# A last group's attention with its own buffers, and contexts dealt out over four steps instead of three

## The chip, the cores and the metric

The kernel runs on one core of a Trainium2 chip. The metric is the device time of one execution in microseconds (us). Times in the profile count from the first instruction of the profiled execution. Engines are called PE (TensorE), PEld (its weight loads), DVE (VectorE), ACT (ScalarE), POOL (GpSimd) and SP (the queue that issues all transfers here).

## The reference

Two layers follow each other on x of 16 batches x 128 tokens x 512 channels; a second input, the context, has the same shape. The first layer is an RWKV block: layer norm, token shift with five learned mixes, projections r, k, v, w, g, a decaying state recurrence per head, group norm, gate, output projection Wo, and a feed-forward part with Wfk, Wfr, Wfv. The second layer is cross attention of each batch with its context:

```python
Mn = conv1x1(Wn, bn, inorm(x_c))
Mm = conv1x1(Wm, bm, inorm(x_s))
A = softmax(einsum('bct,bcs->bts', Mn, Mm), axis=-1)
Ml = conv1x1(Wl, bl, x_s)
Mo = einsum('bcs,bts->bct', Ml, A)
return conv1x1(Wo, bo, Mo) + x_c
```

Here the token index is the channel of the convolution (128) and the 512 channels are positions, so that the scores of one batch are 512 x 512. All arithmetic is in 32-bit floats.

## The kernel before, in words

The 16 batches form 8 groups of two (g = 0 to 7, `n` = 2). The work on a group is cut into stages, each a Python generator that traces a piece and yields: B (line 227: first norm and mixes), B2 (line 268: projections), R (line 358: the recurrence), C (line 568: output projection, second norm, feed-forward: the "output block"), X (line 759: load of the prepared context) and L (line 810: cross attention, two `stageLb` at line 772, one for each batch). The projected context of each batch, Mm and the values side by side, does not depend on the first layer. `context` (line 732) computes it early, and stores it in DRAM (`mvD`); X loads it later.

Steps set the order (line 845 on). In step s, group g is in the stage whose offset in `OFF` (line 27) is s - g: B, B2, R, C, then L and X. So group 0's output block is traced in step 3, group 1's in step 4. `interleave` (line 823) merges the streams of a step by a key, start delay (`DLY`, line 29) plus progress. The contexts of the groups that `EARLY` (line 30) lists for a step are a stream with delay 1 (line 857): they come after most of that step's other work. The last group (g = 7) has streams of its own in step 10: `stageCb` and `stageLb` for each batch (lines 847 to 850).

What is traced is then scheduled by the framework: a planner walks through its own estimate of time and gives each engine a fixed queue, taking what is ready, first the work that was traced first. A tile gets a buffer of its tag when one is free; an instruction that writes it waits until the previous owner's readers are done. So the tags tie stages together:

- In `stageLb` (line 772) for each of four blocks of 128 score rows (`tt`): scores `pS` (line 785), their negated maximum (787), exp into `e` (789), reciprocal (790), scaling (791), four transposes into `pA` (794), and the copy into `AT` (797), which holds two blocks. After every second block `pO` (803) multiplies AT with the values, and line 805 adds the result to x; line 807 stores the batch. `e` has two buffers, `AT` one, the normalized input `l1n` one (line 727), for both batches and all groups. PSUM banks are given by `T` (line 47): tags bx, c and lv have two banks, ls and la one. In the last group batch 0 takes c for pS, ls for pA and lv for pn and pO; batch 1 takes lv, la and bx.
- `context` (line 732) takes xs in yT or xk2 (by batch), its result MVe in xcT or sx2, the normalized copy in `e`, and the banks ls and la. `stageC` uses yT, xk2, xcT and sx2 too (lines 574 to 587), each with one buffer, and kk in yT (line 615).

Of the kernel before, what the change touches and what calls it, by code (L numbers as in the profile page):

```python
# [7 lines left out]
FP = mybir.dt.float32  # L8
# [11 lines left out]
G = B // n  # L20
# [6 lines left out]
OFF = [0, 1, 2, 3, 4, 4]  # L27
ORDER = [3, 4, 2, 1, 0, 5]
DLY = [-0.2, 0.2, 0.0, 0.4, 0.8, 0.4]
EARLY = {0: [0, 1], 1: [2, 3], 2: [4, 5, 6, 7]}  # L30
LASTX = 2


# [1 line left out]
def rwkv_xattn_kernel(ctx: ExitStack, tc: tile.TileContext, a: dict, out: bass.AP):  # L35
# [5 lines left out]
    sb = ctx.enter_context(tc.tile_pool(name="sb", bufs=2))  # L41
    sb1 = ctx.enter_context(tc.tile_pool(name="sb1", bufs=1))
# [4 lines left out]
    def T(tag, g=None, last=None):  # L47

        if g == G - 1 and last:
            tag = last  # L50
        return dict(tag=tag, bufs=PSB[tag])
# [72 lines left out]
    def rownorm(dst, xap, tag, how, ssum=None):  # L124

        sm = lambda nm, w=1: small.tile([128, w], FP, name=nm, tag=tag + nm)
        rs, nb = sm("rs"), sm("nb")
        lin = lambda o, i, scale, bias: nc.vector.tensor_scalar(o, i, scale, bias, ALU.mult, ALU.add)  # L128
        if how == "dve":
            st6, mv = sm("st6", 6), sm("mv", 2)  # L130
            nc.vector.bn_stats(st6, xap)
            nc.vector.bn_aggr(mv, st6)
            lin(nb, mv[:, 0:1], -1.0, 0.0)
            lin(rs, mv[:, 1:2], 1.0, EPS)
        else:
            if ssum is None:
                ssum = sm("su")
                nc.scalar.activation(dst, xap, AF.Identity, accum_out=ssum)
            lin(nb, ssum, -1.0 / E, 0.0)
            sq = sm("sq")  # L140
            nc.scalar.activation(dst, xap, AF.Square, bias=nb, accum_out=sq)
            lin(rs, sq, 1.0 / E, EPS)
        D["pow"] = nc.gpsimd.tensor_tensor(rs, rs, mhalf[:, 0:1], ALU.pow).ins  # L143
        nc.vector.tensor_tensor(nb, nb, rs, ALU.mult)
        nc.scalar.activation(dst, xap, AF.Identity, bias=nb, scale=rs)
# [33 lines left out]
    def center_wv():  # L179
        for m2 in range(2):  # L180
            wvs = sb.tile([128, 2, 512], FP, name="wvs", tag="wb")
            nc.sync.dma_start(out=wvs, in_=a["Wv"][m2])
            wv = wvs.rearrange("p m (h j) -> p (m h) j", j=16)
            mj = sb1.tile([128, 64], FP, name="mj", tag="AT")
            nc.vector.tensor_reduce(mj, wv, AX.X, ALU.add)
# [541 lines left out]
    def inorm(xap, tag, how, ssum=None, tile_=dict(tag="l1n", bufs=1)):  # L727
        xn = sb.tile([128, 512], FP, name="l1n", **tile_)
        rownorm(xn, xap, tag, how, ssum)
        return xn  # L730
# [21 lines left out]
    def stageE(gs):  # L752

        for g in gs:
            for b in range(n):
                context(g, b)
                yield
# [14 lines left out]
    def stageLb(g, b):  # L772
        d = D[g]
        xb = d["x"][b]
        mv = d["MV"][b]
        Mm, Vc = mv[:, 0:512], mv[:, 512:1024].rearrange("p (c t) -> p c t", c=4)
        xh = inorm(xb, "xh", "act", d["ssum"][b])
        pn = ps.tile([128, 512], FP, name="pn", **T("ls", g, ("lv", "bx")[b]))
        nc.tensor.matmul(pn, lhsT=WnT, rhs=xh, start=True, stop=True)
        Mn = sb.tile([128, 512], FP, name="Mn")  # L780
        nc.scalar.activation(Mn, pn, AF.Identity, bias=l1b[:, 0:1])
        for tt in range(4):
            tsl = slice(128 * tt, 128 * tt + 128)
            pS = ps.tile([128, 512], FP, name="pS", **T("ls", g, ("c", "lv")[b]))
            nc.tensor.matmul(pS, lhsT=Mn[:, tsl], rhs=Mm, start=True, stop=True)  # L785
            nm = small.tile([128, 3], FP, name="nm")
            nc.vector.tensor_reduce(nm[:, 0:1], pS, AX.X, ALU.max, negate=True)  # L787
            e = sb.tile([128, 512], FP, name="e")
            nc.scalar.activation(e, pS, AF.Exp, bias=nm[:, 0:1], accum_out=nm[:, 1:2])  # L789
            nc.vector.reciprocal(nm[:, 2:3], nm[:, 1:2])  # L790
            nc.scalar.activation(e, e, AF.Identity, scale=nm[:, 2:3])  # L791
            pA = ps.tile([128, 4, 128], FP, name="pA", **T("la", g, ("ls", "la")[b]))
            for sc in range(4):
                nc.tensor.transpose(pA[:, sc], e[:, 128 * sc : 128 * sc + 128], ident)  # L794
            if tt % 2 == 0:
                AT = sb1.tile([128, 4, 256], FP, name="AT")
            nc.scalar.copy(AT[:, :, 128 * (tt % 2) : 128 * (tt % 2) + 128], pA)  # L797
            if tt % 2 == 0:
                yield
                continue  # L800
            pO = ps.tile([128, 256], FP, name="pO", **T("la", g, ("lv", "bx")[b]))
            for sc in range(4):
                nc.tensor.matmul(pO, lhsT=Vc[:, sc], rhs=AT[:, sc], start=sc == 0, stop=sc == 3)  # L803
            sl = slice(128 * tt - 128, 128 * tt + 128)
            nc.vector.scalar_tensor_tensor(xb[:, sl], pO, cb, xb[:, sl], ALU.add, ALU.add)  # L805
            yield
        nc.sync.dma_start(out=out[n * g + b], in_=xb)
        yield

    def stageL(g):  # L810
        gens = [stageLb(g, b) for b in range(n)]
        while gens:
            for q in list(gens):
                for _ in range(2):
                    try:
                        next(q)
                    except StopIteration:
                        gens.remove(q)
                        break
                yield  # L820
# [24 lines left out]
    for step in range(G + max(OFF)):  # L845
        streams = []
        if step == G + 2:
            for b in range(n):
                streams.append((stageCb(G - 1, b), 6, 0.4 + 0.1 * b, (7 + b, G - 1)))
                streams.append((stageLb(G - 1, b), 3, 1.4 + 0.1 * b, (9 + b, G - 1)))  # L850
        for k in ORDER:
            for g in range(G):
                if step_of(k, g) == step and not (g == G - 1 and k in (3, 4)):
                    streams.append((ST[k][0](g), ST[k][1], DLY[k], (k, g)))
        if step in EARLY:
            gs = EARLY[step]
            streams.append((stageE(gs), 2 * len(gs), 1, (6, step)))
        interleave(streams)
# [71 lines left out]
```

## Time and profile before

| what | value |
|---|---|
| median of 3 runs (lowest, highest) | 971.24 us (967.41, 981.34) |
| profiled execution: its own time, its span | 969.33 us, 967.5 us |
| mean granted TensorE clock | 0.981 |
| busy: PE, DVE, ACT, POOL | 93%, 67%, 52%, 6% of the span |
| DMA | 134.04 MB, mean 139 GB/s |
| context loads (line 737) | 16, issued from 13.5 to 128.8 us |
| context stores (line 749) | 16, issued from 23.8 to 157.6 us |
| last group's attention, first norm to last add | 922.9 to 964.5 us |

The span is from the first to the last instruction; the execution's own time has some start and end around it. A group of the profile gives the number of instructions, their mean duration and what ended the idle time of their engine. "Busy tenths" are 40 equal slices of the span. The chain that ended last goes back from the last instruction, each time to what released it. A matmul of 32-bit floats can have two records, so that one score product shows as x2.

### The profile page before, as it was taken

The numbers are of one execution on the slowest core, as the hardware profiler recorded it, in microseconds if no ns is written. First come the engines' busy times: TensorE is split into PE (matmuls) and PEld (weight loads), VectorE is DVE, ScalarE is ACT, GpSimd is POOL, SyncE is SP. The second block draws the span as 40 slices with busy tenths as digits, with TensorE's granted clock in tenths as the row PEclk, the third lists the DMA queues.
The fourth block names the chain that finished last, engine by engine and source line by source line (L and its number), as shares of the span: only waits on it lengthen the run. The fifth ranks groups of instructions, "written<-read, shape, count | busy, mean of one in ns | idle before, by whom it ended". The sixth has DMA issues, their size and how long they took to land.

```text
span 967.5 us, 19263 instructions
## 1 busy us (share of the span) xinstructions
PE 898.5 (93%) x7556; PEld 613.0 (63%) x7556; DVE 644.3 (67%) x1599; ACT 500.4 (52%) x1057; POOL 59.2 (6%) x95
## 2 busy tenths in 40 slices
PE   4889999998989999999999999999989998997985
PEld 3666767667554867576756677585846565754643
DVE  5787677946586668875787578755784595942322
ACT  4675273443366445564565445734564265654544
POOL 5111010000000000010000000000000000000000
PEclk9999999999999999999999999999999999998998
DMA  6566647355413635253444524553445323344410
GB/s 200 182 239 215 200 154 247 96 158 190 142 55 72 206 123 179 60 173 110 140 115 132 190 86 131 147 182 102 131 112 145 139 66 113 96 155 142 152 44 23
DMA packets 77612, 134.04 MB, mean 139 GB/s; under 512 B 33825, under 2 KB 43681, under 8 KB 77520
## 3 DMA queue, kind: packets, MB, share of 16 engines
q1 hardware_dynamic: 77522, 132.81, 44.5%
q8 instruction: 60, 0.98, 0.4%
q14 instruction: 30, 0.25, 0.1%
HBM read 104.45 MB, written 22.04 MB: 131 GB/s over the span
## 4 chain that ended last, share of the span: by engine, by line
PE 64%; DVE 18%; ACT 7%; DMA 6%; SPq 3%; issue 2%; POOL 0%; DVEq 0%; ACTq 0%; POOLq 0%
PE ptk L594 14%; PE pj L224 11%; PE pv L331 5%; PE pj L621 5%; PE pO L803 4%; PE pl L456 4%; PE pS L785 4%; DVE PP L394 3%; PE pA L794 2%; PE ptl L674 2%; SPq L425 2%; DVE xm L289 2%; PE pu L505 1%; DVE xm L290 1%; PE po L533 1%
## 5 line engine op out<-in xcount | busy, mean ns | idle before, releaser
L224 PE MATMUL pj<-xm,wb 128*128 128x256 f32 x768 | 179.4, 386 | 2.9 <-DVE xm L289 2.8
L224 PEld LDWEIGHTS pj<-xm,wb 128*128 128x128 f32 x768 | 145.3, 193 | 28.3 <-issue 5.7
L143 POOL TENSOR_TENSOR rs<-rs,mhalf 128x1 f32<-128x1 f32 x64 | 40.8, 644 | 619.2 <-DVE rs L128 605.0
L785 PE MATMUL pS<-MV,Mn 128*128 128x512 f32 x112 | 62.9, 644 | 9.1 <-ACT e L789 5.2
L789 ACT ACTIVATE e<-pS,nm 128x512 f32<-128x512 f32 x64 | 44.3, 693 | 50.1 <-DVE nm L787 49.8
L787 DVE TENSOR_REDUCE nm<-pS 128x1 f32<-128x512 f32 x64 | 43.5, 685 | 40.1 <-PE pS L785 39.9
L803 PE MATMUL pO<-AT,MV 128*128 128x256 f32 x224 | 58.4, 399 | 1.9 <-ACT AT L797 1.9
L289 DVE TENSOR_TENSOR xm<-px,sx 128x512 f32<-128x512 f32 x80 | 53.6, 681 | 7.6 <-PE px L286 7.5
L331 PE MATMUL pv<-wb,xm 128*128 128x512 f32 x128 | 57.5, 597 | 0.2 <-DMA wb<-wvc 0.2
L797 ACT COPY AT<-pA 128x512 f32<-128x512 f32 x64 | 37.4, 585 | 39.1 <-PE pA L794 34.7
L791 ACT ACTIVATE e<-e,nm 128x512 f32<-128x512 f32 x64 | 46.4, 730 | 18.7 <-DVE nm L790 18.7
L290 DVE TENSOR_TENSOR xm<-xm,xaT 128x512 f32<-128x512 f32 x80 | 54.4, 684 | 0.5
L803 PEld LDWEIGHTS pO<-AT,MV 128*128 128x128 f32 x224 | 43.1, 198 | 17.8 <-issue 7.1
L621 PE MATMUL pj<-xk,wb 128*128 128x256 f32 x224 | 52.4, 383 | 0.0
L594 PE MATMUL ptk<-wb,kk 128*128 128x512 f32 x112 | 51.4, 596 | 0.9 <-DMA wb<-in_Wfv_dram 0.9
L456 PE MATMUL pl<-KX,r 128*32 128x128 f32 x1536 | 48.6, 274 | 3.3 <-DMA KX<-ks 3.0
L594 PE MATMUL ptk<-wb,sx 128*128 128x512 f32 x112 | 50.8, 598 | 0.0
L594 PE MATMUL ptk<-wb,yT 128*128 128x512 f32 x112 | 49.8, 596 | 0.8 <-DVE nm L790 0.8
L456 PEld LDWEIGHTS pl<-KX,r 128*32 128x32 f32 x1536 | 40.8, 110 | 14.1 <-issue 8.8
L794 PEld LDWEIGHTS pA<-ident,e 128*128 128x128 f32 x256 | 30.0, 141 | 30.6 <-issue 14.0
L805 DVE SCALAR_TENSOR_TENSOR x<-pO,cb,x 128x256 f32<-128x256 f32 x32 | 15.4, 480 | 49.5 <-PE pO L803 49.3
L286 PE MATMUL px<-sk,w2s 98*128 98x256 f32 x160 | 41.7, 356 | 5.4 <-ACT sk L264 2.0
(201 smaller groups left out, 1709.9 us busy)
## 6 DMA issues: line engine op xcount, KB each, us to landing
wb<-in_Wk_dram SPq DMA_DIRECT2D x16, 512.0 KB, 4.6
mvD<-MVe SPq DMA_DIRECT2D x16, 512.0 KB, 4.1
wb<-in_Wr_dram SPq DMA_DIRECT2D x16, 512.0 KB, 3.4
wb<-wvc SPq DMA_DIRECT2D x16, 512.0 KB, 3.6
wb<-in_Wg_dram SPq DMA_DIRECT2D x16, 512.0 KB, 4.2
wb<-in_Wo_dram SPq DMA_DIRECT2D x14, 512.0 KB, 3.4
wb<-in_Wfk_dram SPq DMA_DIRECT2D x14, 512.0 KB, 3.5
MV<-mvD SPq DMA_DIRECT2D x14, 512.0 KB, 3.8
```

Of the source, the lines that this page charges most:

```text
L224: nc.tensor.matmul(pj[:, m], lhsT=wb[:, m, cc, :], rhs=xm[:, cc], start=cc == 0, stop=cc == 3)
L289: nc.vector.tensor_tensor(xm[:, sl], px.rearrange("p c (b t) -> p c b t", b=n), sx[:, sl], ALU.mult)
L290: nc.vector.tensor_tensor(xm[:, sl], xm[:, sl], xaT[:, sl, :, 1:129], ALU.add)
L331: nc.tensor.matmul(pv, lhsT=xm[:, m, b], rhs=wbs[m // 2][:, m % 2], start=m == 0, stop=m == 3)
L456: nc.tensor.matmul(t[cs, 128 * cc : 128 * cc + 128], lhsT=r[:, cc, b, cs], rhs=KX[:, n * cc + b, :, 16 * c : 16 * c + 16], start=True, sto ...
L594: nc.tensor.matmul(pt, lhsT=act[:, m, b], rhs=wbs[m // 2][:, m % 2], start=m == 0, stop=m == 3)
L621: nc.tensor.matmul(pj[:, m], lhsT=wb[:, m, cc, :], rhs=xk2[:, cc], start=cc == 0, stop=cc == 3)
L785: nc.tensor.matmul(pS, lhsT=Mn[:, tsl], rhs=Mm, start=True, stop=True)
L789: nc.scalar.activation(e, pS, AF.Exp, bias=nm[:, 0:1], accum_out=nm[:, 1:2])
L791: nc.scalar.activation(e, e, AF.Identity, scale=nm[:, 2:3])
L794: nc.tensor.transpose(pA[:, sc], e[:, 128 * sc : 128 * sc + 128], ident)
L803: nc.tensor.matmul(pO, lhsT=Vc[:, sc], rhs=AT[:, sc], start=sc == 0, stop=sc == 3)
```

## The change

Two edits are made together. In the last group each batch's `stageLb` takes other buffers: the normalized input goes to tag vt (two buffers), `e` to xm for batch 0 and k for batch 1 (two buffers each), `AT` to at for batch 0 and w for batch 1 (one each). These tags belong to stages that the last group has left by then. All other groups keep e, AT and l1n. And the contexts, which were computed in steps 0 to 2 for 2, 2 and 4 groups, are computed in steps 0 to 3 for 1, 2, 3 and 2 groups. What is computed stays the same, and no instruction is added or taken away.

```diff
-EARLY = {0: [0, 1], 1: [2, 3], 2: [4, 5, 6, 7]}
+EARLY = {0: [0], 1: [1, 2], 2: [3, 4, 5], 3: [6, 7]}
...
-        xh = inorm(xb, "xh", "act", d["ssum"][b])
+        own = lambda tag, *rest: dict(tag=rest[b]) if g == G - 1 else dict(tag=tag)
+        xh = inorm(xb, "xh", "act", d["ssum"][b], *([dict(tag="vt")] if g == G - 1 else []))
...
-            e = sb.tile([128, 512], FP, name="e")
+            e = sb.tile([128, 512], FP, name="e", **own("e", "xm", "k"))
...
-                AT = sb1.tile([128, 4, 256], FP, name="AT")
+                AT = sb1.tile([128, 4, 256], FP, name="AT", **own("AT", "at", "w"))
```

## The prediction

> **What bounds the kernel now.** I read the page first: how much each engine does, and in which of the 40 slices (24.2 us each).
>
> ```profile
> span 967.5 us, 19263 instructions
> ...
> PE 898.5 (93%) x7556; PEld 613.0 (63%) x7556; DVE 644.3 (67%) x1599; ACT 500.4 (52%) x1057; POOL 59.2 (6%) x95
> ...
> PE   4889999998989999999999999999989998997985
> DVE  5787677946586668875787578755784595942322
> ```
>
> TensorE is the bound, except at the two ends: 4, 8, 8 at the start and 7, 9, 8, 5 at the end. The change touches just these ends, so next I read busy time by stretches (columns: PE, PEld, DVE, ACT, POOL, then granted clock, DMA share, GB/s).
>
> ```profile
> 300.00:860.00 560.00, 547.74 (x5043) 375.20 (x5042) 393.17 (x943) 296.56 (x628) 21.16 (x40) 0.99 0.43 130
> ...
> 260.00:270.00 10.00, 10.00 (x137) 8.22 (x136) 4.99 (x16) 6.00 (x14) 0.99 (x1) 1.00 0.36 92
> 270.00:280.00 10.00, 7.28 (x48) 4.11 (x46) 9.88 (x27) 5.33 (x12) 0.93 (x1) 0.94 0.28 95
> 280.00:290.00 10.00, 8.52 (x45) 4.63 (x48) 9.67 (x24) 5.96 (x14) 0.00 (x0) 0.89 0.00 0
> ...
> 930.00:940.00 10.00, 6.57 (x20) 2.80 (x19) 3.82 (x12) 6.18 (x14) 0.55 (x1) 1.00 0.07 26
> 940.00:950.00 10.00, 6.72 (x32) 4.22 (x31) 3.10 (x7) 5.50 (x11) 0.00 (x0) 1.00 0.00 1
> 950.00:960.00 10.00, 6.35 (x30) 4.17 (x28) 2.15 (x6) 5.30 (x12) 0.00 (x0) 1.00 0.08 28
> 960.00:967.50 7.50, 3.27 (x9) 2.07 (x8) 0.48 (x1) 0.58 (x1) 0.00 (x0) 0.59 0.09 35
> ```
>
> Three things are to be seen. From 300 to 860 PE is busy 98%, so whatever the front gains or loses is carried to the end nearly whole. Around 270 to 290 VectorE, not PE, is full. And in the tail no engine is full: the last group's attention waits on itself. The timeline of the tail shows on what (start, duration, engine, line; in brackets the idle time before and its releaser):
>
> ```profile
> 941.42 0.58 ACT L797 COPY AT<-pA 128x512 f32<-128x512 f32 x1 [0.87 <-PE pA L794]
> 942.06 1.59 PEld L803 LDWEIGHTS pO<-AT,MVl 128*128 128x128 f32 x8 [0.91 <-ACT AT L797]
> ...
> 944.09 0.48 DVE L805 SCALAR_TENSOR_TENSOR x<-pO,cb,x 128x256 f32<-128x256 f32 x1 [4.56 <-PE pO L803]
> 944.14 0.59 ACT L797 COPY AT<-pA 128x512 f32<-128x512 f32 x1 [2.14 <-PE pO L803]
> ...
> 960.74 3.20 PE L803 MATMUL pO<-AT,MVl 128*128 128x256 f32 x8 [0.68 <-ACT AT L797]
> ```
>
> At 944.14 the copy into AT is ready (its transposes ended at 941.4) but stands until batch 0's pO matmuls have read the only AT buffer. The same happens at 956.10, again 2.14 us. The view of tile AT has it in one line, among what its engine sat idle before it for (us, times):
>
> ```profile
>   PE pO L803: 4.3, 2
> ```
>
> Last, the chain that ended last, at the front: contexts' work lies on it (start, duration, what).
>
> ```profile
> 27.41 0.69 DVE st L131
> ...
> 40.80 0.86 PE pm L741 x2
> ```
>
> **The change, part by part.**
>
> *Tail: own e, AT and l1n.* No instruction is added; only buffer waits go. l1n: batch 0's pn matmul (925.70) had released it before batch 1's norm began (930.77, just after its sum at 930.5), so this costs and gains nothing; and the new buffers were last used long before (vt at 848, k at 836, w at 781, at at 858, gt2l in xm at 869), so they add no wait. AT: 2 x 2.14 = 4.3 us of ScalarE waits disappear. e: between 938.5 and 944.1 DVE stands, in front of the pO result, though a score tile had been ready since 934.4; with two e buffers for two batches its exp could not have run. ScalarE is busy 17.57 us of the 33.7 between 930.77 and the last add at 964.46, PE 22.91 us of the 37.5 after 930.
>
> Bounds. The best is PE back to back: the 22.91 us include 0.5 before 930.5 and end at 930.5 + 22.4 = 952.9, then one add of 0.48: 953.4, so at most 11.1 us less. The worst without another mechanism is 0: the PSUM tags lv and c, the order of DVE's queue and the chain of one tile (score 1.1, maximum 0.7, exp 0.9, scale 0.7, transposes 0.7, copy 0.6, pO 2.0, add 0.5: 7.2 us) stay. I take 6: the 4.3 measured on AT, and about a quarter (1.7) of the 6.8 left to the best bound for e. What is late next are the score tiles of batch 1, which share the two lv banks with pO of batch 0.
>
> The row for the clock: the last eight pO matmuls took 3.20 us where those before took 2.00, at a granted clock of 0.59 in that stretch, after an idle time of 2.55 us on PE (959.41). A denser tail may win these 1.2 us back, 961.1 in place of 962.3, but I keep them in the sum. [...]
>
> *Front: contexts 4, 4, 8, 0 in steps 0 to 3 become 2, 4, 6, 4.* One context is, by the rows of tile xs, l1n and MVe: on SP a 256 KB load (3.3 us to landing) and a 512 KB store (4.1); on DVE 0.69 + 0.17 + 3 x 0.15 = 1.3 us; on POOL one power, 0.55; on ACT 0.81 + 0.69 + 0.59 = 2.1; on PE 0.86 + 0.89 = 1.75 (chain pieces). Nothing is added in total. Where each move counts:
> - Step 0 loses two contexts. PE is idle there, so their PE time is worth nothing; on the chain are their statistics at 27.41 (0.69) and 29.55 (0.60) and two aggregates (0.08, 0.09): 1.4 us less. Behind them wait the xm products of the first projection (28.10 to 34.7, also DVE), so it is passed on. Bounds 0 and -1.5.
> - Step 1 swaps two for two: nothing, as count and place are the same.
> - Step 2 loses two. From 60 to 160 PE is busy 95.6 us of 100, so at best 2 x 1.75 = 3.5; at least 0, if DVE (160 to 190 full) stays the limit of the first state update. The chain holds 2.3 us of context work there (0.58 at 129.46, 0.89 at 137.88, 0.86 at 143.09). I take half the best: -1.8.
> - Step 3 gains four, which use yT, xk2, xcT and sx2 at the same time as group 0's output block. kk (the yT buffer) is read last by the Wfv matmuls that end at 261.3, sx2 at 262.1. So the four contexts run in two rounds from 261.3 on, and group 1's output block waits for them: before, its yT was written at 287.95, its xcT at 318.65. Fast row: the first context of all held xs 13.47 to 21.2 (7.7 us) and its store landed at 23.77 + 4.1, 14.4 us in all; two rounds free yT at 277 and xcT at 290, both in time. Slow row: between the loads of 96.14 and 125.30 one xs buffer was held 29.2 us; two such rounds free yT at 319.7, 31.7 us late. As to engines: DVE has 5 us free in 260 to 270 and none in 270 to 290, so I put two contexts' 1.3 us each on the path less a little cover, +2.2 (bounds 0 and +31.7); I stay near the fast row, since the slow one stood in a step 2 where PE was full, and PE has idle time after 270; PE's 7.0 us find 4.2 us idle in 270 to 290 and stand beside DVE. POOL is busy 1.9 us of 40 there, so four powers fit. The eight moved transfers find DMA shares of 0.36, 0.28 and 0.00; on SP's queue a load that waits for yT would have the VX loads (266.25) and Wv loads (268.05) behind it, which the upper bound covers. Group 0's attention (first pn at 270.7) shares the ls and la banks with the contexts and may slip; its end at 378 releases the x load at 380.4, needed after 398, so 12 us are covered.
>
> Front: -1.4 - 1.8 + 2.2 = -1.0.
>
> Sum against the profiled execution's own 969.33 us (span 967.5 and 1.8 around it): 969.33 - 6.0 - 1.0 = 962.3. The runs shown have a median of 971.24, 1.9 above that execution, and reach from 967.41 to 981.34; against it the forecast is -0.9%. About 2% is what a measurement of this kernel can tell from no change: 951.8 and 990.7.
>
> **Rivals.**
> 1. *The contexts in step 3 hold group 1's output block* (ends slower). Place: yT at 287.95. Price: one round of the slow row and one half way between the rows (18.4) free yT at 308.9, 21 us late in place of +2.2: 962.3 + 18.8 = 981.1. For it: DVE at 9.9 and 9.7 of 10, in whose queue each context's statistics stand. Against: 27 us of room, and free PE and DMA. It makes the kernel slower than 969.33 once yT comes over 9.2 us late, at 297.2, two rounds of 18.0 us.
> 2. *The tail does not move*: the wait for AT turns into one for the lv banks or in DVE's order. Tail gain 1 instead of 6: 967.3. For it: DVE's 4.56 us stand in front of pO is an order of the queue, not a buffer. Against: the 2.14 us waits name the buffer.
> 3. *Both ends gain their best*: 969.33 - 11.1 - 1.5 - 3.5 = 953.2. For it: no engine is full in the tail. Against: chain of 7.2 us per tile, DVE full at 270.
>
> **How the numbers follow.** Forecast 0.50 (its own range 957 to 967), rival 1 0.18, rival 2 0.20, rival 3 0.12. For 8 in 10 the range goes from 952 (rival 3 with the clock's 1.2) to 980, which takes in most of rival 1. Faster by over 2% needs a little more than rival 3 with the 1.2 us of clock (952.0): 0.07. Slower by over 2% needs rival 1 with 9.6 us more, nearly the two slow rounds: 0.05. The rest, 0.88, is within.
>
> **What would show it.** Right: no wait of AT on pO in the last 40 us, e exps of both batches back to back, under 28 us from batch 1's last Wfv add to the last pO add (33.6 now); four context loads after 240, group 1's yT at 284 to 290. Wrong: that yT after 297, or the tail as long as before with lv named as releaser.

## The result, and the profile after

The changed kernel takes 979.89 us (median of 20 runs, 975.81 to 987.00) against 973.02 us (20 runs) for the kernel before on the same chips: a ratio of 1.0074 with a 95% interval of 1.0057 to 1.0091. It is slower, by 7.2 us, where 0.9% faster was forecast. That is within the 2% that the prediction took as its limit, and 979.89 us lies at the upper end of its range (952 to 980), but the sign is the other one. Its profiled execution took 976.97 us, 7.6 more than the one before (969.33). Lines from 777 on stand one lower in the new listing (pS 786, exp 790, scale 792, pA 795, AT 798, pO 804, add 806, store 808).

First the page of the kernel after: the span, the busy times, then the slices (24.4 us each) of PE, DVE and PE's clock.

```profile
span 975.2 us, 19255 instructions
...
PE 896.5 (92%) x7556; PEld 615.0 (63%) x7556; DVE 645.1 (66%) x1599; ACT 501.0 (51%) x1057; POOL 60.8 (6%) x95
...
PE   4889888999899999999999999999989998997985
...
DVE  5797767964697657875696668756787575644341
...
PEclk9999997999899999999999999999999999999996
```

PE does the same work (896.5 us, 898.5 before) in a longer span, so the loss is idle time of PE: 78.7 us against 69.0. The PE row has three 8s in slices 5 to 7, where the row before had 9s, and the clock of the last slice is at 6 tenths.

Then the stretches that the prediction looked at (columns: PE, PEld, DVE, ACT, POOL, granted clock, DMA share, GB/s).

```profile
300.00:860.00 560.00, 543.08 (x4926) 370.94 (x4925) 391.40 (x942) 296.45 (x629) 22.01 (x40) 1.00 0.43 128
...
270.00:280.00 10.00, 8.89 (x48) 7.23 (x47) 10.00 (x25) 6.57 (x13) 1.87 (x1) 1.00 0.69 241
280.00:290.00 10.00, 9.60 (x64) 6.06 (x62) 9.72 (x29) 6.92 (x16) 0.75 (x2) 1.00 0.59 193
930.00:940.00 10.00, 9.70 (x38) 5.50 (x37) 3.58 (x12) 8.65 (x18) 0.55 (x1) 1.00 0.07 26
940.00:950.00 10.00, 7.95 (x35) 5.07 (x33) 4.06 (x9) 4.98 (x12) 0.00 (x0) 1.00 0.07 27
950.00:960.00 10.00, 6.77 (x24) 5.31 (x24) 1.95 (x7) 5.98 (x15) 0.00 (x0) 0.66 0.01 2
960.00:975.20 15.20, 7.75 (x22) 5.03 (x22) 1.82 (x4) 2.62 (x6) 0.00 (x0) 0.69 0.09 35
```

Around 270 to 290 PE is now busier than before (8.9 and 9.6 of 10, before 7.3 and 8.5): the four late contexts fit there, as foretold. From 940 on the tail is nearly as empty as it was, and it runs at a clock of 0.66 to 0.69 in its last 25 us.

The tail's timeline after shows on what it waits now (start, duration, engine, line, then the idle time before and its releaser).

```profile
947.67 0.48 DVE L806 SCALAR_TENSOR_TENSOR x<-pO,cb,x 128x256 f32<-128x256 f32 x1 [3.97 <-PE pO L804]
948.21 0.31 PEld L786 LDWEIGHTS pS<-MVl,Mn 128*128 128x128 f32 x2 [0.55 <-DVE x L806]
948.53 2.48 DVE L788 TENSOR_REDUCE nm<-pS 128x1 f32<-128x512 f32 x4 [0.37 <-PE pS L786]
949.25 0.69 ACT L790 ACTIVATE e<-pS,nm 128x512 f32<-128x512 f32 x1 [3.67 <-DVE nm L788]
...
951.92 2.56 ACT L792 ACTIVATE e<-e,nm 128x512 f32<-128x512 f32 x4
...
952.70 1.97 PE L795 MATMUL pA<-ident,e 128*128 128x128 f32 x8 [3.35 <-ACT e L792]
...
955.00 3.78 PE L804 MATMUL pO<-AT,MVl 128*128 128x256 f32 x8 [0.33 <-ACT AT L798]
...
966.05 1.11 PE L795 MATMUL pA<-ident,e 128*128 128x128 f32 x4 [2.61 <-ACT e L792]
...
967.84 3.78 PE L804 MATMUL pO<-AT,MVl 128*128 128x256 f32 x8 [0.68 <-ACT AT L798]
971.66 0.48 DVE L806 SCALAR_TENSOR_TENSOR x<-pO,cb,x 128x256 f32<-128x256 f32 x1 [6.42 <-PE pO L804]
```

Line by line: a score tile of batch 1 (948.21) waits for the DVE add that reads batch 0's pO (947.67), since both use the two lv banks. Then four score tiles come at once: four reductions in a row, four exps, four scales, and PE idles 3.35 us until the first scale is done. After that gap the pO products take 3.78 us instead of the 1.99 us of other rounds. It happens again with the last tile, which comes alone at the end (idle 2.61 us).

The wait for the add is not new. The kernel before has it, just as long (0.55 us), and has the four reductions in a row, too:

```profile
943.89 1.88 PE L785 MATMUL pS<-MVl,Mn 128*128 128x512 f32 x4
944.63 0.31 PEld L785 LDWEIGHTS pS<-MVl,Mn 128*128 128x128 f32 x2 [0.55 <-DVE x L805]
944.95 2.48 DVE L787 TENSOR_REDUCE nm<-pS 128x1 f32<-128x512 f32 x4 [0.37 <-PE pS L785]
948.31 1.27 PE L794 MATMUL pA<-ident,e 128*128 128x128 f32 x8 [2.54 <-ACT e L791]
949.64 2.00 PE L803 MATMUL pO<-AT,MVl 128*128 128x256 f32 x8
```

New is that ScalarE, with the own e buffers, does all four exps before the scales, where it did two and two, so that PE idles 3.35 us in place of 2.54.

The waits that were to go did go. This is the view of tile AT from 920 on, what its engine sat idle before it for (us, times); "PE pO", 4.3 us before, is no longer listed.

```profile
its engine sat idle before it (us, times) until:
  PE pA L795: 8.6, 5
  ACT AT L798: 7.9, 10
  issue: 1.0, 4
```

From the start of batch 1's last Wfv add (line 722) to the start of its last pO add it is 34.2 us before (929.79 to 963.98) and 42.0 after (929.71 to 971.66). In the kernel after, this stretch also holds the end of group 6's attention, whose stores (915.4 and 931.2 before) have moved to 937.0 and 943.7. What that adds is not shown: the tail alone, below, reads 40.9 us with these stores at 923.2 and 937.9, before and just after its batch 1's last Wfv add at 936.4.

At the front, group 1's output block starts on time: its first yT record is at 286.78 (287.95 before; 284 to 290 foretold). What is late is group 0's attention. SP's timeline after:

```profile
380.26 0.36 SPq L808 DMA_DIRECT2D out_dram<-x  x1
...
397.69 0.54 SPq L808 DMA_DIRECT2D out_dram<-x  x1
398.28 4.46 SPq L425 DMA_DIRECT2D KX<-ks  x7
402.79 0.59 SPq L61 DMA_DIRECT2D x<-in_x_dram  x1
```

Its two stores were issued at 361.55 and 378.19 before, and the load of x that follows the second one at 380.40: 19, 20 and 22 us later now. Group 2's yT comes at 396.9 instead of 391.8.

### The profile page after: what moved, and what is told of

It reads as the page before. It is cut to its first block, busy times and chain, and to the rows that moved or that the text cites. A ratio compares the mean times of both kernels' runs of the same rounds, so it can differ in the third digit from the quotient of the medians.

```text
span 975.2 us, 19255 instructions
## 1 busy us (share of the span) xinstructions
PE 896.5 (92%) x7556; PEld 615.0 (63%) x7556; DVE 645.1 (66%) x1599; ACT 501.0 (51%) x1057; POOL 60.8 (6%) x95
## 4 chain that ended last, share of the span: by engine, by line
PE 64%; DVE 14%; DMA 10%; ACT 6%; SPq 4%; issue 2%; POOL 1%; DVEq 0%; ACTq 0%; POOLq 0%
PE ptk L594 12%; PE pj L224 11%; PE pv L331 6%; PE pO L804 5%; PE pj L621 5%; PE pS L786 4%; PE pl L456 4%; DVE PP L394 2%; SPq L425 2%; PE pA L795 2%; PE pu L505 1%; PE ptl L674 1%; PE pa L526 1%; DVE xm L289 1%; DMA s<-in_s_dram 1%
## 5 line engine op out<-in xcount | busy, mean ns | idle before, releaser
L143 POOL TENSOR_TENSOR rs<-rs,mhalf 128x1 f32<-128x1 f32 x64 | 43.6, 688 | 650.3 <-DVE rs L128 638.1
L786 PE MATMUL pS<-MV,Mn 128*128 128x512 f32 x112 | 59.1, 610 | 2.8 <-ACT e L790 2.7
L804 PE MATMUL pO<-AT,MV 128*128 128x256 f32 x224 | 54.7, 384 | 1.2 <-ACT AT L798 1.2
L594 PE MATMUL ptk<-wb,kk 128*128 128x512 f32 x112 | 53.9, 622 | 1.4 <-DMA wb<-in_Wfv_dram 1.4
L804 PEld LDWEIGHTS pO<-AT,MV 128*128 128x128 f32 x224 | 41.2, 190 | 12.1 <-issue 4.8
```

The source lines that it names most:

```text
L594: nc.tensor.matmul(pt, lhsT=act[:, m, b], rhs=wbs[m // 2][:, m % 2], start=m == 0, stop=m == 3)
```

## The experiments

Each was timed beside the kernel before; ratios are to it, with 95% intervals. For each run I also give two readings of its profile: the tail (from batch 1's last Wfv add to its last pO add, starts, as above), and PE's idle time from the start to 180 and to 300 us (the stretch less PE's busy time). The tail reading scatters from profile to profile: six kernels with the tail of before (before, three other deals or delays, two with the Wg edit) read 34.2 to 38.4 us, so only a difference well beyond that says something.

### The two halves

The tail alone is the changed kernel with the old deal:

```diff
-EARLY = {0: [0], 1: [1, 2], 2: [3, 4, 5], 3: [6, 7]}
+EARLY = {0: [0, 1], 1: [2, 3], 2: [4, 5, 6, 7]}
```

> Theory A (the contexts in step 3 delay group 0's attention and all that hangs on it; the tail edit is a gain): the tail alone gives 5 us less than before, ratio about 0.994, all steps up to 860 us as before, last group's attention about 5 us shorter. Theory B (the planner's order is reshuffled by any edit): some shift in either direction, up to 7 us, that starts before the last group.

Measured: ratio 1.0006 (0.9984 to 1.0029). There is no gain at all. Its tail is 40.9 us in the profiled execution (the slowest of its runs, 982.7 us), with the same picture: four reductions, four exps, four scales, 3.35 us of idle PE, then pO products at 3.67 us.

The front alone is the kernel before with the new `EARLY`.

> Theory A: the front alone costs more than the whole change, +12 us, ratio about 1.013: the last group's y comes 13 us late as in the changed kernel, and the tail gives nothing back. Theory B: no fixed sum; front alone and tail alone don't add up to the whole (+7).

Measured: 1.0040 (1.0018 to 1.0062), a loss, but a third of the one expected. Stores of group 0 at 379.9 and 397.4, so the slip comes with the deal and not with the tail's edit. Within the intervals the two halves add up to the whole (1.0046 against 1.0074).

### What bounds the tail

The kernel before with own buffers for AT and the normalized input, e left shared:

```diff
-                AT = sb1.tile([128, 4, 256], FP, name="AT")
+                AT = sb1.tile([128, 4, 256], FP, name="AT", **own("AT", "at", "w"))
```

> Before with own AT buffers and own norm buffers in the last group, e as before. Theory G (own AT takes away 4.3 us of waits; own e makes ScalarE's queue run four exps before four scales, and gives it back): ratio 0.996. Theory H (the two lv banks bound the tail): 1.000.

Measured: 1.0006 (0.9975 to 1.0037), tail 36.6 us. The two waits of 2.14 us were not worth their 4.3 us: even the lower end of the interval is a gain of only 2.4 us. The other way round, own e and normalized input, AT shared:

```diff
-            e = sb.tile([128, 512], FP, name="e")
+            e = sb.tile([128, 512], FP, name="e", **own("e", "xm", "k"))
```

> Before with own e and norm buffers in the last group, AT as before. Theory G: four exps in a row, the waits of AT on pO still there, ratio 1.003 or more. Theory H: 1.000.

Measured: 1.0018 (0.9996 to 1.0040), tail 38.5 us. So neither buffer alone is the bound. Then all of the tail's edits (old deal), and batch 0's pO out of the lv banks:

```diff
-            pO = ps.tile([128, 256], FP, name="pO", **T("la", g, ("lv", "bx")[b]))
+            pO = ps.tile([128, 256], FP, name="pO", **T("la", g, "bx"))
```

> Before with the whole tail edit, and batch 0's pO in the bx banks, so that lv holds scores of batch 1 only. Theory H: score products no longer wait for the add after pO; 4 us or more less, ratio 0.996 or below. Theory G: four exps in a row stay, 1.000.

Measured: 959.66 us, ratio 0.9850 (0.9824 to 0.9877). The tail is 24.5 us. This version beats both kernels. PE's timeline in its tail:

```profile
937.44 1.98 PE L786 MATMUL pS<-MVl,Mn 128*128 128x512 f32 x4 [0.34 <-ACT Mn L782]
940.16 2.84 PE L786 MATMUL pS<-MVl,Mn 128*128 128x512 f32 x6 [0.74 <-ACT e L790]
942.84 1.20 PE L795 MATMUL pA<-ident,e 128*128 128x128 f32 x8
945.08 0.66 PE L795 MATMUL pA<-ident,e 128*128 128x128 f32 x4 [1.04 <-ACT AT L798]
946.23 1.99 PE L804 MATMUL pO<-AT,MVl 128*128 128x256 f32 x8 [0.50 <-ACT AT L798]
948.06 0.60 PE L795 MATMUL pA<-ident,e 128*128 128x128 f32 x4
948.50 1.89 PE L804 MATMUL pO<-AT,MVl 128*128 128x256 f32 x8
950.23 1.04 PE L795 MATMUL pA<-ident,e 128*128 128x128 f32 x8
951.51 0.66 PE L795 MATMUL pA<-ident,e 128*128 128x128 f32 x4 [0.24 <-ACT AT L798]
952.00 3.72 PE L804 MATMUL pO<-AT,MVl 128*128 128x256 f32 x16
```

All the scores are done before the first pO of the stretch; no score tile waits for an add any more. The longest idle gap is 1.04 us, and every eight pO products take 1.86 to 1.99 us; the granted clock is 1.00 from 930 to 950.

Does the bank do it alone? The same pO line in the kernel before, with nothing else changed:

> The kernel before with one edit: batch 0's pO in the last group takes a bx bank instead of lv, so batch 1's scores have both lv banks to themselves; e, AT and the normalized input stay shared. Theory J (the bank alone bounded the tail): most of the 0.985 of the run with both edits comes back, ratio 0.985 to 0.991, and the last add under 957. Theory K (bank and own buffers are needed together, each is hidden behind the other): ratio 0.994 to 1.000, waits of AT on pO of about 2 us are there again.

Measured: 964.75 us, 0.9905 (0.9880 to 0.9929), tail 27.4 us. The bank alone brings about two thirds, inside theory J's ratio, though its last add (960.6 in the profile) is not under 957. Theory K's sign is there too: the AT wait is back (view of AT, what its engine sat idle for):

```profile
  PE pO L803: 2.3, 3
```

So the own buffers are worth about 5 us more (0.9905 to 0.9850, intervals that do not overlap), but only once the bank is free.

A wait of 0.55 us cannot be what 9 us were won from. The order of PE's queue changed with the bank. Before, three of the last group's eight score tiles stand behind batch 0's first pO products: two at 943.89, one at 955.85. With pO in a bx bank all eight stand before them, and no score waits for the add:

```profile
942.18 1.98 PE L785 MATMUL pS<-MVl,Mn 128*128 128x512 f32 x4 [0.74 <-ACT e L789]
944.00 1.25 PE L794 MATMUL pA<-ident,e 128*128 128x128 f32 x8
945.57 1.13 PE L785 MATMUL pS<-MVl,Mn 128*128 128x512 f32 x2 [0.32 <-ACT e L789]
946.53 1.89 PE L803 MATMUL pO<-AT,MVl 128*128 128x256 f32 x8
```

So the shared bank seems to have cost its time mostly through the place that the planner gave the scores, and hardly as a wait.

### The front: late contexts, their banks, their number

No context in step 3 (the changed kernel with the following deal: 2, 4 and 10 contexts in steps 0 to 2):

```diff
+EARLY = {0: [0], 1: [1, 2], 2: [3, 4, 5, 6, 7]}
```

> Contexts for 1, 2, 5, 0 groups in steps 0 to 3, tail as changed. Theory A: no context stands beside group 0's attention, so its end comes at about 378 to 382 again and the ratio is 0.994. Theory C (it is steps 0 and 1, with fewer contexts to fill TensorE's idle time, that lose): still 5 us or more slower than the tail edit alone, ratio 1.000 to 1.007.

Measured: 1.0091 (1.0068 to 1.0114). The last product of a context (pm) begins at 136.6 us, the first product of group 0's attention is at 271.4 (270.9 before), and yet its stores come at 380.3 and 399.6. Contexts in step 3 are not needed for the slip or the loss. Theory A is out, and the loss is larger than theory C had it. The opposite, only step 3's four moved late and the early steps as they were (4, 4, 4, 4):

```diff
+EARLY = {0: [0, 1], 1: [2, 3], 2: [4, 5], 3: [6, 7]}
```

> Contexts for 2, 2, 2, 2 groups in steps 0 to 3, tail as changed: steps 0 and 1 as before, step 3 as changed. Theory A: as slow as the change, ratio 1.005 to 1.01, group 0's attention ends at about 395. Theory C: 0.994.

Measured: 1.0086 (1.0053 to 1.0119), stores at 379.8 and 397.2. This number was met, though the run before says that its reason is not the only one. Next the banks: the new deal alone, with the products of the contexts of groups 6 and 7 in bx, which belong to the projections:

```diff
-        pm = ps.tile([128, 512], FP, name="pm", **T("ls"))
+        pm = ps.tile([128, 512], FP, name="pm", **T("bx" if g >= 6 else "ls"))
-        pV = ps.tile([128, 512], FP, name="pV", **T("la"))
+        pV = ps.tile([128, 512], FP, name="pV", **T("bx" if g >= 6 else "la"))
```

> Front edit alone, but the contexts of groups 6 and 7 (step 3) take the bx banks in place of ls and la. Theory A (they hold ls until 281 us, so that group 0's attention begins at 288 instead of 271 and ends at 397 instead of 378, and that is what costs): first pn back at 271 to 276, end of group 0 at 378 to 385, ratio 1.000 or below, against 1.004 of the front alone. Rival D (the order of the rest, not the banks): first pn earlier, but the ratio stays at 1.003 or more.

Measured: 1.0413 (1.0382 to 1.0444), 1015 us. It tells nothing of ls and la: the projections' banks are worse to share (PE idles 15.8 us between 240 and 300 against 6.5 before, and the last multiply of group 3's group norm, line 559, starts at 522.6 instead of 490.5). The same edit with lv in place of bx:

> The new deal alone, with the products of the contexts of groups 6 and 7 in lv banks, so that group 0's attention has ls and la for itself. Theory A (the banks ls and la, held by the four late contexts from 265 to 286, push group 0's attention back): its first product at about 271, its outputs at 362 and 378, ratio 0.997 to 1.001. Theory I (PE had less to do up to 180 us and its work is owed later, wherever the contexts keep their products): idle time of PE up to 180 still 30 us or more against 23.7, ratio 1.002 to 1.008.

Measured: 1.0085 (1.0055 to 1.0116). Group 0's attention begins at 270.7, as theory A had it, but its stores move only to 374.9 and 390.4, PE's idle time by 180 is 35.0 us, and nothing is won. So a late start for want of ls and la does not explain the loss. The recurrence uses lv as well (line 372), and what sharing it costs is not separated here.

Now the ledger of PE. The busy time by stretches of the kernel before, then of the kernel after:

```profile
60.00:180.00 120.00, 115.33 (x1015) 84.85 (x1015) 94.50 (x244) 58.65 (x120) 9.59 (x15) 0.97 0.64 205
180.00:300.00 120.00, 109.17 (x933) 71.14 (x931) 81.36 (x192) 56.79 (x128) 6.12 (x8) 0.97 0.41 120
```

```profile
60.00:180.00 120.00, 104.48 (x948) 76.84 (x947) 88.94 (x216) 49.42 (x103) 7.87 (x12) 0.94 0.54 170
180.00:300.00 120.00, 111.43 (x964) 76.19 (x964) 85.11 (x211) 59.91 (x130) 9.57 (x12) 0.97 0.49 151
```

Between 60 and 180 us PE has done 10.9 us less than before, and between 180 and 300 only 2.3 more. The chain to group 1's yT is on time, but work is owed, and PE is busy 97 to 98% from 300 to 860. To see whether too few contexts in step 2 cause this, two deals in the kernel before; 2, 6 and 8 contexts, then 4, 6 and 6:

```diff
+EARLY = {0: [0], 1: [1, 2, 3], 2: [4, 5, 6, 7]}
```

> The kernel before with the contexts of one, three and four groups in steps 0 to 2 (2, 6, 8 and 0 contexts): none in step 3, and step 2 keeps its eight. Theory I' (what costs is a step 2 with fewer contexts than eight, since they fill PE's gaps between 120 and 180 us, and what PE doesn't do there is owed later): PE idle between 120 and 180 about 2 us, ratio 0.998 to 1.002. Theory O (the old deal is one order out of many, any other order of the queues costs some tenths of a per cent up to two): 1.004 or more, with idle time elsewhere.

Measured: 1.0019 (0.9988 to 1.0050), PE idle between 120 and 180 1.9 us. No loss that this can tell from none.

```diff
+EARLY = {0: [0, 1], 1: [2, 3, 4], 2: [5, 6, 7]}
```

> The kernel before with one group's contexts moved from step 2 to step 1 (4, 6, 6 and 0 contexts), step 0 as it was. Theory I': PE idle between 120 and 180 us 5 us or more against 2.2, and ratio 1.004 to 1.009, though no context is late. Theory O: a ratio over 1.003 too, but the idle time need not lie between 120 and 180. If only late contexts cost (the banks ls and la held beside group 0's attention): 0.998 to 1.002.

Measured: 1.0024 (0.9997 to 1.0050), idle 3.5 us there. Both readings are under theory I', though the interval reaches into the low end of its range. The last one keeps the deal of before, and only traces the contexts earlier among each step's work, so that the planner finds another order:

```diff
-            streams.append((stageE(gs), 2 * len(gs), 1, (6, step)))
+            streams.append((stageE(gs), 2 * len(gs), 0.5, (6, step)))
```

> The kernel before with its own deal (4, 4, 8 and 0 contexts), only that the stream of contexts has the delay 0.5 in place of 1, so that they are traced among the second half of each step's work instead of behind it, and the planner makes another order of the queues. Theory I' (the number of contexts in step 2 decides): ratio 0.998 to 1.003, PE idle between 120 and 180 us about 2 us. Theory O (the order of the queues decides, whatever the deal): 1.004 or more.

Measured: 979.72 us, 1.0063 (1.0038 to 1.0087), with PE's stretches so:

```profile
60.00:180.00 120.00, 108.04 (x974) 78.45 (x974) 89.26 (x225) 55.33 (x116) 8.21 (x15) 0.94 0.60 193
180.00:300.00 120.00, 109.25 (x930) 77.40 (x929) 79.46 (x183) 48.68 (x105) 4.96 (x8) 0.93 0.43 126
```

With eight contexts in step 2, as before, PE idles 7.1 us between 120 and 180, so their number does not decide. The same deal in another order loses about as much as the new deal, and in the same stretch: 7.3 us less PE work between 60 and 180. All kernels with the old tail bank, in order of idle time by 300:

| kernel | PE idle to 180, to 300 (us) | ratio |
|---|---|---|
| own e alone, old deal | 23.8, 34.1 | 1.0018 |
| tail alone, old deal | 24.6, 34.4 | 1.0006 |
| before | 23.7, 34.6 | 1 |
| own AT alone, old deal | 25.6, 35.5 | 1.0006 |
| 2, 6, 8, 0 | 25.6, 35.8 | 1.0019 |
| before, Wg on GpSimd (below) | 26.7, 37.1 | 0.9999 |
| 4, 6, 6, 0 | 27.3, 37.2 | 1.0024 |
| 4, 4, 4, 4, new tail | 27.7, 38.7 | 1.0086 |
| new deal alone (2, 4, 6, 4) | 31.3, 39.5 | 1.0040 |
| 2, 4, 10, 0, new tail | 27.8, 40.7 | 1.0091 |
| old deal, delay 0.5 | 30.3, 41.0 | 1.0063 |
| delay 0.5, Wg on GpSimd (below) | 29.6, 41.6 | 1.0118 |
| new deal alone, Wg on GpSimd (below) | 33.3, 42.1 | 1.0045 |
| after | 33.9, 42.5 | 1.0074 |
| new deal, late contexts in lv | 35.0, 44.9 | 1.0085 |
| new deal, late contexts in bx | 32.7, 50.9 | 1.0413 |

Cheap orders lie under 38 us, costly ones above, but among the costly ones the loss does not follow the idle time (38.7 us at 1.0086, 42.1 at 1.0045). This is a relation over one profile each, not a law: the control run below, with PE's order unchanged, shows 37.1 us at a ratio of 0.9999, so single profiles differ by some 2.5 us. Nor does the loss end at 300: from 300 to 860 PE idles 12.3 us before, 16.9 after, 18.1 in the new deal alone and 17.2 at delay 0.5.

Not every new order costs, either. The traces show that the deals 2, 6, 8 and 4, 6, 6 also move work about on PE, without a loss clear of noise. Between 60 and 185 us, without the contexts' own products, 82 to 88% of their order agrees with that of the kernel before. In the kernel after, the new deal alone (also with late contexts in lv), 2, 4, 10, 0 and the delay of 0.5 it is 66 to 71%, while among each other these agree to 89% or more. So it looks like one costly order that several edits lead to. The deal 4, 4, 4, 4 is an exception: 81% as before, and yet 1.0086.

Is it one place? The two orders of the new deal (alone, after), the one at delay 0.5 and the one with late contexts in lv share a wait of PE of 1.8 to 3.0 us for group 1's Wg load near 147 to 152 us, which stands in SP's queue behind VX loads; these wait 14.2 us in the kernel after, 11.8 at delay 0.5, and 0.8 in the kernel before. The Wg load on another queue, in the new deal alone:

```diff
-                pj4 = proj("Wg", xm, m2)
+                pj4 = proj("Wg", xm, m2, nc.gpsimd if g == 1 else None)
```

> The new deal alone, with group 1's two loads of Wg issued on GpSimd's queue in place of SP's. Theory Q (in the new deal the VX loads stand at the head of SP's queue for 14 us until the values of group 0 are read, and Wg stands behind them, so PE waits for Wg near 147 us and for the gate product after it): the 1.8 to 2.7 us wait for Wg goes, PE idle up to 180 us falls from 31.3 to 27 or less, ratio at or under 1.002 against 1.004. Theory O (the loss is spread over many places of the order): the ratio stays 1.003 to 1.006, even if this wait goes.

Measured: 1.0045 (1.0019 to 1.0072), PE idle 33.3 us by 180, and the wait is still there, 1.98 us. What its engine sat idle for before the two loads, from the view of tile wb on GpSimd (us, times):

```profile
  DMA VX<-vD: 6.0, 1
  PE pv L331: 1.0, 1
```

The first load was released after a VX load had landed, so this run alone does not clear the VX loads. The second needs the buffer that the Wv products (line 331) read to their end. The edit did not take the wait away. The control, the same edit in the kernel before:

> The kernel before with the same edit of the two Wg loads, as a control: all queues but SP's and GpSimd's keep their order. Wg was not late there, so both theories expect 0.998 to 1.002.

Measured: 0.9999 (0.9978 to 1.0021). And in the order at delay 0.5:

> The old deal with the contexts traced at delay 0.5, and group 1's Wg loads on GpSimd's queue. Theory Q: the wait of 2.7 us for Wg goes and the ratio falls from 1.0063 by 0.003 or more, to 1.003 or less. Theory O: 1.005 to 1.008.

Measured: 1.0118 (1.0087 to 1.0149), more than without the edit; the wait stays (1.87 us), and why the rest got worse is open. Here both loads on GpSimd waited for the Wv products, and for nothing on SP's queue (same view):

```profile
  PE pv L331: 7.0, 2
```

In this order, at least, a late Wg follows from PE's order of products.

### Tail and front together

The whole change with the pO line above:

> The whole change, and batch 0's pO in a bx bank. If the cost of the front and the gain of the tail are separate terms of a sum, 0.985 plus the front's 0.004 to 0.007: ratio 0.988 to 0.993. If the tail's mending also hides the front's loss, 0.985; if the later arrival of group 6's attention fills the tail so that the bank no longer matters, 1.000 or more.

Measured: 967.60 us, 0.9939 (0.9917 to 0.9961), tail 28.3 us. With the bank free the change would have been a gain, but the new deal takes 0.9% of the 1.5% back. A last deal in the mended kernel, with more contexts early:

```diff
+EARLY = {0: [0, 1, 2], 1: [3, 4], 2: [5, 6, 7]}
```

> The mended tail (own buffers, pO in bx), with the contexts dealt out the other way: three, two and three groups in steps 0 to 2 instead of two, two and four. Theory I (the sum of PE's idle time up to 300 us decides what a deal costs: 34 to 36 us idle in the old deal, 39 to 42 in the later ones): two contexts more beside PE's idle time of step 0 leave idle time at 300 no higher, ratio 0.978 to 0.986. Rival (any deal other than the one that the kernel came with costs, because the planner's order changes): 0.990 or more.

Measured: 1.0088 (1.0060 to 1.0116), 2.4% slower than the mended kernel with the old deal, with idle time by 300 of 41.2 against 36.2 us. The rival's number was met. Contexts put where PE is idle in step 0 did not lower the idle time; the new order raised it elsewhere (8.1 us between 120 and 180). But these 5.0 us are the smaller part of the loss: from 300 to 860 PE idles 27.2 us, 14.8 more than in the mended kernel with the old deal.

## Why the prediction was wrong, point by point

- *AT, 2 x 2.14 us.* The waits went, the time did not: own AT alone gave 1.0006. The step that failed is to take 4.3 us of waits for 4.3 us of path. Behind them stood the lv banks, which the prediction itself named as what is late next, and rival 2 as a mechanism. That rival had 0.20; its sign came (a tail at least as long, held by the add that frees lv). The bank's own row, 0.55 us at 944.63, was in the profile before, but so small that it gave no hint of what the bank cost through the order. The tail term was -6.0; measured +0.6 us (-1.6 to +2.8).
- *e, 1.7 us.* Own e lets the four exps and then the four scales run in blocks, so the first transposes wait for four exps. Seen in the timeline after; alone it gave 1.0018. With the bank free, own e, own AT and own l1n together bring 5 us. That this comes near the 6.0 is luck: the AT waits there are 2.3 us in sum, not 4.3, and the shares of the three buffers were not separated.
- *Best bound of the tail.* From the end of the last Wfv add (930.5) to 953.4 it was 22.9 us; the mended kernel needs 24.3 (931.98 to 956.23). The bound was sound, and freeing the bank, which the prediction did not change, came near to it.
- *The clock, 1.2 us.* Kept as no gain, which was a choice. The changed tail kept such gaps: two rounds took 3.78 us, after 3.35 and 2.61 us, at a granted clock of 0.66 to 0.69. The mended one, denser (no gap over 1.04 us), had all rounds at 1.86 to 1.99. So the slow round is gone in the denser tail, and the one after 2.61 us agrees with the row (3.20 us after 2.55). But not every gap of this size does it: in the kernel before, the products after one of 2.54 us (948.31) took 2.00.
- *l1n at nothing.* Not tried by itself: it went along with own AT and with own e.
- *Step 0, step 3.* The chain behaved as foretold: group 1's yT at 286.78, 1.2 us early, 1.0 foretold; the fast row held, with context loads at 229.9, 260.95, 267.96 and 272.30, so that three of the four came after 240, where all four were expected. Rival 1 (that yT after 297) did not come.
- *"12 us are covered".* This step of the front failed. Group 0's attention slipped 19 to 20 us, and its slip was put down to the banks ls and la. Without late contexts, and with them in other banks, the slip remained in good part. What the slip cost is not shown: the x load of 402.79 landed at 406.9, and the add that reads it (line 599) starts at 409.4, behind its product on PE.
- *The front's sum, -1.0.* Measured +3.9 us (+1.8 to +6.0) alone. The step that failed is the credit of 1.4 and 1.8 us for the contexts taken out of steps 0 and 2. The working followed one chain to yT and took removed contexts as time won, with the order of the rest unchanged. In the kernel after, PE had instead done 10.2 us less by 180 (idle 33.9 against 23.7), and won only part back: -2.3 from 180 to 300, +4.7 to 860, -2.9 at the end, in sum the 9.7 us more idle time.
- *The forecast of sign.* What no rival had: that a new deal makes the planner order the queues anew, and that a new order can cost 0.6% by itself. The delay of 0.5 shows it with the deal unchanged (1.0063); the deals 2, 6, 8 (1.0019) and 4, 6, 6 (1.0024) show that not every new order does. That the new deal loses its 0.4% in this way, and not by a place of its own, is likely from the common order, but not shown. Which part of the order makes PE idle is open; the Wg load was one guess, and the run could not take its wait away.

## What to carry to other kernels

When a wait on a buffer is removed, look for the next shared resource of the same stage (here a PSUM bank) and test that one first. The length of its wait is no measure of its cost: 0.55 us of wait stood for 9 us here, because the bank also set the order of PE's queue. On an engine that is full for most of the span, judge a moved piece of work by the engine's busy time as well, and not only by one milestone that stays on time. Where a planner orders the queues, a change of place can change every queue: run the old version in another order once, to know what a new order can cost by itself.

## What the runs showed of the hardware

In these tails PE went at about half its pace after some short gaps. In the tail after, eight pO products took 3.78 us after an idle time of 3.35 us, and again after one of 2.61 us, both times at a granted clock of 0.50 (955.0 to 958.6 and 967.8 to 971.7); the eight between them took 1.99 us at 1.00 (960.6 to 962.4). After gaps up to 1.04 us (the mended tail) eight took 1.86 to 1.99. In all five profiles with a gap of 3.35 us (after, tail alone, own e alone, the deals 2, 4, 10, 0 and 4, 4, 4, 4) the next eight were slow, 3.54 to 3.78 us. At 2.5 to 2.6 us it went both ways: before, 2.00 us after 2.54 and 3.20 after 2.55; in the deal 4, 4, 4, 4, 1.99 after 2.62; at delay 0.5 with Wg on GpSimd, 1.99 after one gap of 2.54 and 3.34 after another. What decides there is open.

The two loads of 512 KB that GpSimd issued (new deal alone) took 0.69 and 0.54 us of its time to issue, where SP's two took 0.33 to 0.37 in the kernel after. They took 4.0 and 6.7 us to land (3.9 and 7.4 in the control), where the 16 loads of Wg on SP's queue took 4.2 (median, on the page before).
